# A list scheduler that tracks ScalarE's function table: an attention layer and a four-way selective scan on one core

## The chip, the core and the metric

The kernel runs on one core of one Trainium2 chip. The metric is the device time of one execution in microseconds (us). Five kinds of queues work side by side: PE (TensorE, matmuls and transposes, with its weight loads shown as PEld), DVE (VectorE), ACT (ScalarE), POOL (GpSimd), and SP, which here only issues DMAs. Each queue runs its instructions strictly in the order in which they were written, and waits on semaphores where an input or a buffer is not ready. The order in each queue is therefore the whole schedule.

## The reference, cut to what matters

Layer 0 is attention over a 256 x 256 grid of tokens with 128 channels: for each of the 256 rows, four heads of 32 channels attend along the row with a mask and a triangle bias, with a sigmoid gate, an output projection and a residual. Layer 1 is a selective scan in four directions over the same grid:

```python
xz = einsum('bhwc,ec->bhwe', x, in_proj_w); xin, z = split(xz, 2)
xc = silu(depthwise_conv3x3(xin) + conv_b)              # 256 channels
xs = [rows, columns, rows reversed, columns reversed]    # four directions k
dts_r, Bs, Cs = split(einsum('bkdl,kcd->bkcl', xs, x_proj_w))
dt = softplus(einsum('bkrl,kdr->bkdl', dts_r, dt_proj_w) + dt_proj_b)
# per direction k, channel d (256) and state n (16), along 65536 tokens:
h = h * exp(dt * A[k, d, n]) + (dt * xs) * B[n]
y = sum over n of h * C[n]
# then: sum of the directions, D * xs, layer norm, times silu(z), out_proj, residual
```

A group norm stands in front of either layer.

## The kernel before, in words

**Layer 0** works in 64 groups of 4 rows. Per row: PE makes the scores of the four heads (`scores`, L557), DVE adds the bias and takes the minimum of the negated sums (`soften`, L576), ACT takes the exponential with its row sum (`exponent`, L590), PE transposes the result (L628), ACT or DVE copies it to SBUF (L373), PE multiplies with v (L646, L651), and DVE gates (L659, L660). Per group, ACT takes one sigmoid for the gates (L509), which needs another function table than the exponential.

**Layer 1** runs the directions in the order 0, 2, 1, 3. A direction is 64 chunks of 1024 tokens, and a chunk is 32 units: 16 states times two halves of 128 channels. A unit u is:

- decay: ACT takes `exp(dt * A)` for 128 x 1024 (L1721);
- bx: `dtu * B` for each state, in eight 128 x 256 pieces a chunk and state, on ACT (L1335) or POOL (L1337), whichever is free; PE transposes the pieces into one of two PSUM buffers (`feed`, L1741);
- scan: DVE runs the recurrence over 1024 tokens (L1787);
- carry: the last state is copied out for the next chunk, on ACT (L1812) or DVE (L1814);
- hc: the states times C, on POOL or on DVE (both L1805). Which of the two is decided when the scan is placed (`choose`): if POOL's queue is short, the scan writes to SBUF and POOL multiplies ("pooled"); else the scan writes to PSUM and DVE multiplies;
- add: PE transposes the product and adds it into y (L1824); `closing` and `open_group` pass y from one group of units to the next, with a copy by ACT between them (`part`, L1377; `ys`, L1382), and sums of earlier results (`part` and `yl`, L1407).

In direction 0, half of the states instead let POOL make `xu * B` (`fill`, L1762), and ACT writes the decay to PSUM. Beside the units, each chunk has work that prepares a later chunk or finishes an earlier one: in direction 0 the convolution (L1093) and its silu (L1111); in all directions dt's projection (L1219), its softplus (L1237), transposes (L1297) and products (L1305); in direction 3 the final part: statistics (L1556, L1557), the normalisation of eight blocks on ACT (L1587) or POOL (L1592), z (L1526), its silu (L1543), the transposes of y (L1607) with their copies (`yn`, L1615), the gate's product on POOL (L1630), the output projection (L1641) and the residual (L1651).

ACT's functions lie in tables of which one is loaded at a time. A silu or softplus between decays thus costs a load before it and another before the next decay. Copies, scalings and identities need no load. The loads are not in the source; they are put in where the finished order of ACT needs them. In the source such a silu or softplus is a task of the kind `visit` (`visit1` for direction 3's silu).

The order of all queues comes from `Play`, a list scheduler that runs while the program is built. It keeps a time for each queue. `COST` gives each kind of task how long it occupies its queue and when its result is there. `pick` looks at each queue's available tasks, takes those that can start within `close` of the first, and among these the one with the smallest `due`; `step` places it. Due times are counted in units (a decay of unit u in direction 3 is due at u - 2, a feed at u - 2, and so on, from the table `TUNE`), so neither `due` nor `COST` is a time on the chip. A task with two queues (`bx` pieces, the normalisations, layer 0's copies) goes to the one where it can start first. `room` and `Lazy` bound how many buffers of a kind are in use. The tasks are only ordered by the play: on the chip each instruction starts when its queue and its semaphores allow.

Of the kernel before, what the change touches and what calls it, by code (L numbers as in the profile page):

```python
# [60 lines left out]
def _normalise(nc, out, in_, mr):  # L61
# [6 lines left out]
    "scan": (2.25, 2.34), "dve_c": (1.15, 1.23), "stat": (1.06, 1.1), "small": (0.15, 0.2),  # L68
    "add": (0.60, 0.68), "last": (0.08, 0.16),
    "decay": (1.045, 1.15), "scale": (0.402, 0.50), "carry": (0.085, 0.19), "e512": (0.47, 0.58),  # L70
    "e1024": (0.90, 1.0), "e128": (0.15, 0.25), "xn": (1.25, 1.35), "visit": (4.93, 3.62), "visit1": (4.64, 3.35), "xp": (1.05, 1.15), "dscale": (0.30, 0.40), "pool_d": (0.31, 0.36), "diag8": (1.76, 1.95),
    "norm_p": (0.91, 0.95), "give": (1.78, 1.95), "shift": (0.55, 0.65),
    "norm": (0.98, 1.1), "a512": (0.67, 0.78),
    "pool": (2.335, 2.38), "pool_s": (0.453, 0.49), "pool_x": (1.26, 1.3), "rstd": (2.0, 2.1),
    "turn8": (0.885, 1.05), "mm": (0.87, 1.05), "dp": (1.0, 1.15), "turn4": (0.45, 0.62),
    "turn_b": (0.67, 0.85), "dma": (0.36, 1.6), "dma2": (0.72, 3.2),
    "d512": (0.60, 0.69), "n512": (0.62, 0.81), "t256": (0.34, 0.42), "og": (0.76, 0.85),
    "soft": (0.85, 0.95), "exp2": (0.90, 1.0), "gate": (3.85, 2.60), "bias": (4.54, 4.55),
    "bc": (0.62, 0.70), "four": (0.95, 1.25), "dma3": (1.0, 1.6),
}  # L80


class Task:
# [3 lines left out]
class Play:  # L87
# [4 lines left out]
    def __init__(self):  # L92
        self.free_at = dict.fromkeys(self.ENGINES, 0.0)
        self.avail = {e: [] for e in self.ENGINES}
        self.close = 0.12
        self.moved = 0.0

    @staticmethod
    def after_own(d):
# [2 lines left out]
    def task(self, eng, cost, due, emit, deps=(), gate=None, more=0, lag=0.0):  # L102

        t = Task()
        t.eng = (eng,) if isinstance(eng, str) else eng
        t.cost = (cost,) if isinstance(cost, str) else cost
        t.due, t.emit, t.gate, t.after, t.by = due, emit, gate, [], None
        t.ready, t.left, t.lag = 0.0, more, lag
        for d in deps:
            if d.by is None:  # L110
                d.after.append(t)
                t.left += 1
            else:
                t.ready = max(t.ready, self.after_own(d) if t.eng == (d.by,) else d.end + SEM)
        if t.left == 0:
            self.offer(t)
        return t
# [5 lines left out]
    def sp(self, due, emit, deps=(), gate=None, cost="dma"):  # L123
        return self.task("SP", cost, due, emit, deps, gate)

    def pick(self):

        best = None
        for e in self.ENGINES:
            f, can, first = self.free_at[e], [], None  # L130
            for t in self.avail[e]:
                r = max(t.ready + t.lag if t.lag and e != t.eng[0] else t.ready, f)
                if t.gate is not None:
                    g = t.gate()
                    if g is None:
                        continue
                    r = max(r, g)
                can.append((r, t))
                first = r if first is None else min(first, r)
            if first is None or (best is not None and first > best[0]):  # L140
                continue
            due, r, t = min(
                ((t.due, r, t) for r, t in can if r <= first + self.close), key=lambda x: x[:2]
            )
            if best is None or r < best[0]:
                best = (r, t, e)
        return best

    def step(self):

        best = self.pick()
        if best is None:
            return False
        now, t, e = best
        occupied, latency = COST[t.cost[t.eng.index(e)]]
        for x in t.eng:
            self.avail[x].remove(t)
        if e == "SP":
            self.moved = max(self.moved, now + LEAD) + latency
            latency = self.moved + LAND - now  # L160
        t.by, t.fin, t.end = e, now + occupied, now + latency
        self.free_at[e] = t.fin
        t.emit(t)
        for x in t.after:
            x.left -= 1
            x.ready = max(x.ready, self.after_own(t) if x.eng == (e,) else t.end + SEM)
            if x.left == 0:
                self.offer(x)
        return True
# [563 lines left out]
def _layer1(tc, ctx, const, dram, ident, vec, mr, a, x1, x1T, out):  # L733
# [93 lines left out]
    xn = const.tile([P, LR + 2, N + 2], F32, tag="xn", name="xn")  # L827
# [8 lines left out]
    SU = ND * ST  # L836
# [25 lines left out]
    task, sp, avail, free_at = play.task, play.sp, play.avail, play.free_at  # L862
# [5 lines left out]
    def direction():  # L868
        return work[min(scanned // SU, len(work) - 1)][0]
# [4 lines left out]
    TUNE = {  # L874
        0: dict(
            w=7, hc=3, c=4, b=2, xu=3, dt=2, dtuT=1, bx=5, pull=(0.2, 1.5, 3), most=4, fills=1.5,
            calm=3, close=0.3, piece=-3.0, decay=-0.7, feed=-1, fill=-3, times=2.2, add=2.5, carry=0.8,
            early=0.0, conv=(-40.0, 5.0, 0.0), side=2.0, again=3, last=0,
            fed=(0, 2, 4, 6, 8, 10, 12, 14),
        ),  # L880
        1: dict(
            w=5, hc=4, c=5, b=3, xu=1, dt=2, dtuT=1, bx=8, pull=(-0.3, 1.5, -1), most=12, fills=2.5,
            calm=4, close=0.2, piece=-9.0, decay=-2, feed=-2, fill=-1.8, times=1.2, add=1.2, carry=1.2,
            early=0.0, conv=(-40.0, 4.5, 0.5), side=-1.0, again=0, last=0.6, fed=(), xs=1,
        ),
        2: dict(
            w=5, hc=3, c=6, b=3, xu=1, dt=2, dtuT=1, bx=8, pull=(-0.3, 1.5, -1), most=8.0, fills=4.5,
            calm=4, close=0.08, piece=-9.0, decay=-2, feed=-2, fill=-1.8, times=0.3, add=2.5, carry=0.8,
            early=0.0, conv=(-40.0, 4.5, 0.5), side=2.0, again=3, last=0, fed=(), xs=1,
        ),  # L890
        3: dict(
            w=6, hc=4, c=4, b=3, xu=1, dt=2, dtuT=1, bx=8, pull=(0.2, 1.5, -2), most=12.0, fills=5.5,
            calm=4, close=0.12, piece=-9.0, decay=-2, feed=-2, fill=-0.8, times=3, add=4, carry=1.2,
            early=0.0, conv=(-40.0, 4.5, 0.5), side=2.0, again=3, last=0.3, fed=(), xs=1,
        ),
    }
# [95 lines left out]
    def calm(u):  # L992

        def gate():
            ahead = min(u, scanned + TUNE[direction()]["calm"])
            return 0.0 if decayed >= ahead else None

        return gate
# [39 lines left out]
    def prep(i):  # L1038

        k, o, cc = chunk(i)  # L1040
        U = SU * i + TUNE[k]["side"]
# [9 lines left out]
        if k == 0:  # L1051
# [35 lines left out]
            outs = []  # L1087
            for x, j in enumerate((1, 0)):
                for q in range(QT):
# [8 lines left out]
                    def leave(pc, j=j, q=q):  # L1098
# [6 lines left out]
                        gate=xu.gate, first=xu.get, gap=c2,  # L1105
# [6 lines left out]
                        xu.half[j], xu.half[j], AF.Silu, bias=vec["conv_b"][:, j : j + 1]  # L1112
                    )

            have = [[task("ACT", "visit", U - 22, silu, outs, calm(SU * i))]] * 2
            kept = [sp(U - 18, store_xc, have[0], None, "dma2")]
            w["stores"] += kept
        else:
            xs = w["xs"] = Lazy("xs", 2, k) if k == 3 else Lent()
# [4 lines left out]
            have = [[], []]  # L1124
# [749 lines left out]
    with tc.manual_schedule():  # L1874
        n_prep, n_pieces, n_units = 0, 0, 0
        while True:
            while n_prep < len(work) and scanned >= SU * n_prep - 60:
                prep(n_prep)
                n_prep += 1
            while n_pieces < 2 * len(work) and scanned >= 16 * n_pieces - 28:  # L1880
                make_pieces(*divmod(n_pieces, 2))
                n_pieces += 1
            while n_units < min(total, scanned + 14):
                make_unit(n_units)
                n_units += 1
            play.close = TUNE[direction()]["close"]
            if not play.step():
                break
        assert scanned == total and all(x.left == 0 for x in [groups[len(work) - 1, 2]["out"]])
        assert play.done()  # L1890

@with_exitstack
def kernel(ctx: ExitStack, tc: tile.TileContext, a, out):
# [32 lines left out]
    with ExitStack() as l0:  # L1926
# [47 lines left out]
```

## Time and profile before

| what | value |
|---|---|
| median of 3 runs | 24744.65 us (24725.2 to 24746.45) |
| profiled execution | 24753.32 us, its span 24751.6 us |
| granted TensorE clock, mean | 0.982 |
| first scan of directions 0, 2, 1, 3 | at 2140.5, 8063.5, 13380.3, 18726.1 us |
| end of the last scan | 24717.1 us |
| scans (L1787) | 8192, 2.33 to 2.34 us each |
| hc on POOL and on DVE (L1805) | 6255 of 2376 ns, 1937 of 1223 ns |
| bx pieces on ACT and on POOL | 19751 of 502 ns, 8921 of 483 ns |
| decays (L1721) | 8192, 1116 to 1148 ns |
| table loads of ACT | 898 of 1283 ns |

Successive ACT instructions overlap by about 0.1 us, so 502 ns of one bx piece is about 0.40 us of ACT's time when many follow each other. A line of the profile gives the engine, the source line, what was written and read, how often, the busy time and the mean of one, and then the idle time of the engine before it with what ended it. The releaser is inferred: it is the one of several that the profile saw last, and where the named engine had long been done, it was another. A line number below is one of the kernel before; the changed kernel's are higher by 13 from `step` on.

### The profile page before, as it was taken

The page shows a single profiled execution, that of the slowest core. Times are in us where ns is not written, and L with a number is a line of the kernel's source. Part 1 is how long each engine was busy: PE and PEld are TensorE (multiplying, and loading weights), DVE is VectorE, ACT ScalarE, POOL GpSimd, SP SyncE. Part 2 cuts the span into 40 slices and gives each one's busy share as a digit, 9 for nine tenths or more (in the row PEclk, how much of TensorE's full clock was granted, in tenths as well). Part 3 has the DMA queues.
Part 4 walks back from the last instruction along what each step waited for, and adds up shares of the span by engine and source line. Part 5 has one row for each costly group of instructions (what it writes and reads, how often), then busy time and mean ns, then how long its engine had stood idle before and what let it go on. Part 6 is the DMA issues. An engine that isn't in the chain of part 4 may idle for free. (4 is left out here: it accounts for less than half of the span.)

```text
span 24751.6 us, 464821 instructions
## 1 busy us (share of the span) xinstructions
PE 23003.9 (93%) x165172; PEld 18188.1 (73%) x165172; DVE 23434.1 (95%) x19272; ACT 23427.6 (95%) x46416; POOL 23325.3 (94%) x17424
## 2 busy tenths in 40 slices
PE   8999999999999999999999999999998888888888
PEld 6666666666666788888887777777777777777777
DVE  7887999999999999999999999999999999999999
ACT  7998899999998999999999999999999999999998
POOL 5777999999999999999999999999999999999999
PEclk9999999999999999999999999999999999999999
DMA  4225777777777666666666777777775555555555
GB/s 131 90 90 171 255 259 264 259 260 262 261 259 255 233 233 225 232 228 229 231 230 232 243 245 243 244 243 244 244 243 198 180 184 178 181 182 181 185 178 168
DMA packets 2471853, 5355.13 MB, mean 216 GB/s; under 512 B 177121, under 2 KB 1366424, under 8 KB 2469528
## 3 DMA queue, kind: packets, MB, share of 16 engines
q1 hardware_dynamic: 2469240, 5324.34, 64.0%
q8 instruction: 1305, 21.38, 0.4%
q14 instruction: 1020, 8.36, 0.1%
q0 software_dynamic: 288, 1.05, 0.0%
HBM read 4846.54 MB, written 478.15 MB: 215 GB/s over the span
## 5 line engine op out<-in xcount | busy, mean ns | idle before, releaser
L1805 POOL TENSOR_TENSOR hc<-w,c 128x1024 f32<-128x1024 f32 x6255 | 14726.7, 2376 | 529.5 <-DVE w L1787 195.1
L1787 DVE TENSOR_TENSOR_SCAN w<-w,hst,s 128x1024 f32<-128x1024 f32 x5550 | 12670.6, 2329 | 295.0 <-PE s L1741 143.8
L1824 PE MATMUL y<-ident,hc 128*128 128x128 f32 x65536 | 8478.1, 277 | 520.8 <-ACT part L1377 204.8
L1741 PE MATMUL s<-ident,bx 128*128 128x128 f32 x57344 | 7713.6, 279 | 1020.7 <-DVE w L1787 662.0
L1741 PEld LDWEIGHTS s<-ident,bx 128*128 128x128 f32 x57344 | 6428.1, 142 | 3009.5 <-DVE w L1787 1289.0
L1335 ACT ACTIVATE bx<-dtuT,bT 128x256 f32<-128x256 f32 x19751 | 8578.3, 502 | 2.8 <-PE s L1741 2.5
L1824 PEld LDWEIGHTS y<-ident,hc 128*128 128x128 f32 x65536 | 7445.2, 142 | 1407.1 <-POOL hc L1805 598.2
L1721 ACT ACTIVATE w<-dt,negA 128x1024 f32<-128x1024 f32 x7168 | 8126.5, 1148 | 31.3 <-PE y L1824 15.8
L1337 POOL TENSOR_SCALAR bx<-dtuT,bT 128x256 f32<-128x256 f32 x8921 | 4103.7, 483 | 22.6 <-ACT dtuT L1034 5.9
L1787 DVE TENSOR_TENSOR_SCAN s<-w,hst,s 128x1024 f32<-128x1024 f32 x1618 | 3775.7, 2338 | 310.1 <-PE s L1741 205.7
L1805 DVE TENSOR_TENSOR hc<-s,c 128x1024 f32<-128x1024 f32 x1937 | 2366.2, 1223 | 101.6 <-DVE s L1787 27.5
L1762 POOL TENSOR_TENSOR w<-xu,b 128x1024 f32<-128x1024 f32 x1024 | 2423.2, 2372 | 0.5 <-issue 0.4
L1093 PE MATMUL cv<-xn,wtap 128*128 128x512 f32 x4608 | 2217.6, 600 | 5.5 <-ACT xn L1080 5.5
L1787 DVE TENSOR_TENSOR_SCAN w<-s,hst,w 128x1024 f32<-128x1024 f32 x705 | 1642.3, 2337 | 58.8 <-ACT s L1721 55.1
L538 POOL TENSOR_TENSOR bias<-tri,mk 128x2048 f32<-128x2048 f32 x256 | 1167.1, 4559 | 378.8 <-DVE nm L576 218.2
L1812 ACT COPY hst<-w 128x1 f32<-128x1 f32 x6255 | 1138.1, 185 | 276.7 <-DVE w L1787 244.7
L1721 ACT ACTIVATE s<-dt,negA 128x1024 f32<-128x1024 f32 x1024 | 1143.0, 1116 | 89.1 <-DVE hc L1805 88.1
L1093 PEld LDWEIGHTS cv<-xn,wtap 128*128 128x128 f32 x4608 | 790.1, 193 | 529.4 <-issue 523.2
L1219 PE MATMUL dp<-xd,dtw 8*128 8x512 f32 x2048 | 1169.4, 662 | 5.2 <-ACT xd L1189 0.9
L590 ACT ACTIVATE s<-s,nm 128x256 f32<-128x256 f32 x2048 | 1028.3, 515 | 0.8
L576 DVE CUSTOM_DVE_ANT_0 s<-sp,bias 128x256 f32<-128x256 f32 x2048 | 754.4, 415 | 69.1 <-PE sp L557 61.1
L1787 DVE TENSOR_TENSOR_SCAN s<-s,hst,w 128x1024 f32<-128x1024 f32 x319 | 745.2, 2336 | 67.4 <-POOL w L1762 67.4
(183 smaller groups left out, 19594.3 us busy)
## 6 DMA issues: line engine op xcount, KB each, us to landing
c<-xp_d SPq DMA_DIRECT2D x7040, 512.0 KB
b<-xp_d SPq DMA_DIRECT2D x896, 512.0 KB
yrow_d<-ys SPq DMA_DIRECT2D x128, 1024.0 KB
yl<-yrow_d SPq DMA_DIRECT2D x512, 256.0 KB
xc_d<-xu SPq DMA_DIRECT2D x128, 512.0 KB
yl<-xc_d SPq DMA_DIRECT2D x128, 512.0 KB
xu<-xc_d SPq DMA_DIRECT2D x128, 512.0 KB
xcT_d<-wtap SPq DMA_DIRECT2D x128, 512.0 KB
```

Of the source, the lines that this page charges most:

```text
L538: nc.gpsimd.tensor_tensor(z["bias"].get(), tri.rearrange("p b h k -> p (b h) k"), w["mk"].tile.rearrange("p (r k) -> p r k", k=N)[:, r : r ...
L1093: return lambda pc: nc.tensor.matmul(pc, wtap[:, j, t, :], xn[:, 2 * q + u : 2 * q + u + 2, v : v + N], start=t == 0, stop=t == 8,)
L1219: return lambda pt: nc.tensor.matmul(pt, dtw[:, k, j, :], xd.half[0][0:R, q * 512 : (q + 1) * 512], start=True, stop=True,)
L1335: nc.scalar.mul(dst, src, b)
L1337: nc.gpsimd.tensor_scalar(dst, src, b, 1.0, ALU.mult, ALU.mult)
L1721: nc.scalar.activation(dst, w["dt"].half[j], AF.Exp, scale=negA[:, k * ND + j, n : n + 1])
L1741: nc.tensor.transpose(dst[:, x * P : (x + 1) * P], blocks(half)[:, x, :], ident)
L1762: nc.gpsimd.tensor_tensor(box["w"].half[0], w["xu"].half[j], b_now().half[0], ALU.mult)
L1787: nc.vector.tensor_tensor_scan(rev(states), rev(a), rev(b), hst[k][:, j, n : n + 1], ALU.mult, ALU.add)
L1805: eng.tensor_tensor(box["hc"].half[0], states, c_now().half[0], ALU.mult)
L1812: nc.scalar.copy(dst, src)
L1824: nc.tensor.matmul(gr["y"][:, x, :], hc[:, x * P : (x + 1) * P], ident, is_transpose=True, start=gr["fresh"] and x == 4 * q, stop=stop and ...
```

## The change

Four things change, all of them in what the play knows and in its numbers. No operation of the reference's computation is added or removed.

1. The play keeps the table that ACT has loaded (`self.table`). `TABLE` names the table of a decay, a `visit` (softplus), a `visit0` (the convolution's silu, a new kind) and a `visit1`. Where the next task of ACT needs another table, `LOAD` = 1.41 is added to its time, and it may start that much earlier than its inputs are there.
2. The kinds `visit` and `visit1` no longer contain two loads: (4.93, 3.62) becomes (2.10, 2.21), and (4.64, 3.35) becomes (1.82, 1.93).
3. In layer 0, three kinds get other numbers: `soft` 0.85 to 0.69, `exp2` 0.90 to 0.985, `four` 0.95 to 1.07. The kind `six` is added to the table and used by no task.
4. Some due times and `close` in `TUNE` change, in each of the four directions.

```diff
-    "visit": (4.93, 3.62), "visit1": (4.64, 3.35),
+    "visit": (2.10, 2.21), "visit0": (2.10, 2.21), "visit1": (1.82, 1.93),
...
-    "soft": (0.85, 0.95), "exp2": (0.90, 1.0),
+    "soft": (0.69, 0.79), "exp2": (0.985, 1.09),
...
-    "four": (0.95, 1.25), "dma3": (1.0, 1.6),
+    "four": (1.07, 1.35), "six": (1.335, 1.6), "dma3": (1.0, 1.6),
 }
+
+LOAD = 1.41
+TABLE = {"decay": "exp", "visit": "softplus", "visit0": "silu", "visit1": "silu"}
...
         self.moved = 0.0
+        self.table = None
...
+    def load(self, e, t):
+        if e != "ACT" or TABLE.get(t.cost[t.eng.index(e)], self.table) == self.table:
+            return 0.0
+        return LOAD
+
     def pick(self):
...
                     r = max(r, g)
+                r = max(r - self.load(e, t), f)
                 can.append((r, t))
...
         occupied, latency = COST[t.cost[t.eng.index(e)]]
+        now += self.load(e, t)
...
         t.by, t.fin, t.end = e, now + occupied, now + latency
+        if e == "ACT":
+            self.table = TABLE.get(t.cost[t.eng.index(e)], self.table)
         self.free_at[e] = t.fin
...
         0: dict(
-            calm=3, close=0.3, piece=-3.0, decay=-0.7, feed=-1, fill=-3, times=2.2, add=2.5, carry=0.8,
+            calm=3, close=0.3, piece=-3.0, decay=-0.7, feed=-1.5, fill=-3, times=2.2, add=2.5,
+            carry=0.8,
...
         1: dict(
-            calm=4, close=0.2, piece=-9.0, decay=-2, feed=-2, fill=-1.8, times=1.2, add=1.2, carry=1.2,
-            early=0.0, conv=(-40.0, 4.5, 0.5), side=-1.0, again=0, last=0.6, fed=(), xs=1,
+            calm=4, close=0.2, piece=-9.0, decay=-2, feed=-2, fill=-1.8, times=2.2, add=2.5, carry=1.2,
+            early=0.0, conv=(-40.0, 4.5, 0.5), side=-1.0, again=0, last=0.3, fed=(), xs=1,
...
         2: dict(
-            calm=4, close=0.08, piece=-9.0, decay=-2, feed=-2, fill=-1.8, times=0.3, add=2.5, carry=0.8,
+            calm=4, close=0.08, piece=-9.0, decay=-2, feed=-2, fill=-1.8, times=0.3, add=3.2, carry=0.8,
...
         3: dict(
-            calm=4, close=0.12, piece=-9.0, decay=-2, feed=-2, fill=-0.8, times=3, add=4, carry=1.2,
+            calm=4, close=0.2, piece=-9.0, decay=-2, feed=-2, fill=-0.8, times=3, add=4, carry=1.2,
...
-            have = [[task("ACT", "visit", U - 22, silu, outs, calm(SU * i))]] * 2
+            have = [[task("ACT", "visit0", U - 22, silu, outs, calm(SU * i))]] * 2
```

What the two built programs hold, counted from their instruction orders:

| | before | after |
|---|---|---|
| hc on DVE, directions 0, 2, 1, 3 | 768, 342, 383, 444 | 769, 342, 384, 504 |
| bx pieces on ACT, directions 0, 2, 1, 3 | 4073, 5475, 5271, 4932 | 4079, 5478, 5190, 4448 |
| normalisations of direction 3 on ACT and on POOL | 262, 250 | 500, 12 |
| DVE's places that differ, layer 0 and directions 0, 2, 1, 3 | | 1697 of 6050; 25 of 3588; 6 of 2988; 789 of 2687; 891 of 3961 |
| table loads of ACT | 898 | 898 |

More of the change, by code (lines that the diff above doesn't have):

```diff
@@ L70 @@
     "decay": (1.045, 1.15), "scale": (0.402, 0.50), "carry": (0.085, 0.19), "e512": (0.47, 0.58),
-    "e1024": (0.90, 1.0), "e128": (0.15, 0.25), "xn": (1.25, 1.35), "visit": (4.93, 3.62), "visit1": (4.64, 3.35), "xp": (1.05, 1.15), "dscale": (0.30, 0.40), "pool_d": (0.31, 0.36), "diag8": (1.76, 1.95),
+    "e1024": (0.90, 1.0), "e128": (0.15, 0.25), "xn": (1.25, 1.35), "visit": (2.10, 2.21), "visit0": (2.10, 2.21), "visit1": (1.82, 1.93), "xp": (1.05, 1.15), "dscale": (0.30, 0.40), "pool_d": (0.31, 0.36), "diag8": (1.76, 1.95),
     "norm_p": (0.91, 0.95), "give": (1.78, 1.95), "shift": (0.55, 0.65),
@@ L77 @@
     "d512": (0.60, 0.69), "n512": (0.62, 0.81), "t256": (0.34, 0.42), "og": (0.76, 0.85),
-    "soft": (0.85, 0.95), "exp2": (0.90, 1.0), "gate": (3.85, 2.60), "bias": (4.54, 4.55),
-    "bc": (0.62, 0.70), "four": (0.95, 1.25), "dma3": (1.0, 1.6),
-}
+    "soft": (0.69, 0.79), "exp2": (0.985, 1.09), "gate": (3.85, 2.60), "bias": (4.54, 4.55),
+    "bc": (0.62, 0.70), "four": (1.07, 1.35), "six": (1.335, 1.6), "dma3": (1.0, 1.6),
+}
+LOAD = 1.41
+TABLE = {"decay": "exp", "visit": "softplus", "visit0": "silu", "visit1": "silu"}
 class Task:
@@ L876, in _layer1 @@
             w=7, hc=3, c=4, b=2, xu=3, dt=2, dtuT=1, bx=5, pull=(0.2, 1.5, 3), most=4, fills=1.5,
-            calm=3, close=0.3, piece=-3.0, decay=-0.7, feed=-1, fill=-3, times=2.2, add=2.5, carry=0.8,
-            early=0.0, conv=(-40.0, 5.0, 0.0), side=2.0, again=3, last=0,
+            calm=3, close=0.3, piece=-3.0, decay=-0.7, feed=-1.5, fill=-3, times=2.2, add=2.5,
+            carry=0.8, early=0.0, conv=(-40.0, 5.0, 0.0), side=2.0, again=3, last=0,
             fed=(0, 2, 4, 6, 8, 10, 12, 14),
```

## The prediction

> **What bounds the kernel now.** I read the page's totals first, then a table of windows cut at the first scan of each direction, then the waits of single stages, and last the timeline around the longest of those waits.
>
> ```profile
> PE 23003.9 (93%) x165172; PEld 18188.1 (73%) x165172; DVE 23434.1 (95%) x19272; ACT 23427.6 (95%) x46416; POOL 23325.3 (94%) x17424
> ```
>
> Four engines stand within 2% of each other, so no engine alone is "the" bound: a microsecond moved from one to another comes back. What can be won is idle time, and of that DVE has 24751.6 - 23434.1 = 1317 us in all. The windows (layer 0 with the start of layer 1, then directions 0, 2, 1, 3 in the order in which they run) show where it lies:
>
> ```profile
> 0.00:2140.50 2140.50, 2008.52 (x17832) 1394.76 (x17832) 1666.58 (x6050) 1870.39 (x5587) 1420.78 (x592) 0.99 0.34 99
> 2140.50:8063.50 5923.00, 5742.90 (x31957) 3968.10 (x31956) 5652.90 (x3589) 5347.45 (x9196) 5666.38 (x2460) 0.95 0.75 259
> 8063.50:13380.30 5316.80, 4974.28 (x38645) 4277.57 (x38644) 5193.14 (x2989) 5259.37 (x10278) 5223.85 (x4424) 0.99 0.69 229
> 13380.30:18726.10 5345.80, 4977.73 (x37099) 4086.75 (x37097) 5234.16 (x2688) 5230.15 (x10503) 5224.84 (x4600) 1.00 0.72 244
> 18726.10:24751.60 6025.50, 5300.51 (x39644) 4460.93 (x39644) 5687.36 (x3961) 5720.20 (x10856) 5789.49 (x5351) 0.98 0.54 180
> ```
>
> The columns after the length are busy PE, weight loads, DVE, ACT, POOL. DVE idles 270 us in direction 0, 124 in direction 2, 112 in direction 1 and 338 in direction 3. Scans follow each other in a fixed order on DVE, so a scan that starts late is the lost time. In layer 0, ACT leads: between 180 and 2060 us nearly all its idle time is the last line below, 0.97 us for each of the 64 groups. The lines before it are DVE's and POOL's waits in direction 3 (waiter, line waited for, us in total, times, longest):
>
> ```profile
> DVE s L1787 <- ACT w L1721: 100.6, 61, 1.7
> DVE w L1787 <- ACT bx L1335: 33.1, 12, 2.9
> DVE w L1787 <- ACT w L1721: 25.6, 15, 2.1
> ...
> POOL wtap L1630 <- ACT hst L1812: 94.3, 58, 2.9
> ...
> ACT e L373 <- PE pT L628: 61.9, 64, 1.8
> ```
>
> 61 times in 64 chunks is once a chunk. I numbered the scans inside a chunk 0 to 31 (S28 is scan 28, f28 the transposes of L1741 that feed it, a28 its transposes of L1824 into y, d28 its decay on ACT, h28 its product with C, c28 its carry). The 100.6 us are all at S28; 80.7 us (1.26 a chunk) are at S13, and 23.4 at S14. Here is PE, then DVE, before one S28:
>
> ```profile
> 21706.56 1.06 PE L1824 MATMUL y<-ident,hc 128*128 128x128 f32 x8 [0.43 <-ACT hst L1812]
> 21707.46 1.88 PE L1407 MATMUL y<-part,ident 128*128 128x512 f32 x4
> 21709.18 0.60 PE L1297 MATMUL dtp<-ident,dt 128*128 128x128 f32 x4
> 21709.62 1.88 PE L1407 MATMUL y<-yl,ident 128*128 128x512 f32 x4
> 21711.34 1.91 PE L1741 MATMUL s<-ident,bx 128*128 128x128 f32 x16
> ...
> 21712.47 2.35 DVE L1787 TENSOR_TENSOR_SCAN s<-w,hst,s 128x1024 f32<-128x1024 f32 x1 [1.67 <-ACT w L1721]
> ```
>
> The wait is put down to ACT, but f28 (the first half of the x16) ends at about 21712.4, right before the scan: f28 stands in PE's queue behind the part sums, a dt transpose and the yl sums. S13 has the same shape:
>
> ```profile
> 21756.43 0.99 ACT L1377 COPY part<-y 128x1024 f32<-128x1024 f32 x1
> ...
> 21757.57 1.06 PE L1824 MATMUL y<-ident,hc 128*128 128x128 f32 x8 [2.35 <-ACT part L1377]
> ...
> 21758.47 1.68 PE L1407 MATMUL y<-yl,ident 128*128 128x512 f32 x2
> ...
> 21759.93 1.91 PE L1741 MATMUL s<-ident,bx 128*128 128x128 f32 x8
> ...
> 21761.94 2.35 DVE L1787 TENSOR_TENSOR_SCAN w<-w,hst,s 128x1024 f32<-128x1024 f32 x1 [2.12 <-ACT w L1721]
> ```
>
> The part copy frees y, a8 opens it again, a yl sum goes first, then f13, then the scan.
>
> **The change part by part.** I laid the two programs' instruction orders side by side, engine by engine.
>
> *Table loads.* Both programs hold 382 loads before decays, 256 before softplus, 64 before each of the two silus: 766 in layer 1, so none is saved. A visit was played as 4.93 us; now it is 2.10 + 2 x 1.41 = 4.92. Only the second load's place differs: it is charged at the next decay, not at the visit. Row: a load takes 1283 ns and the next activation starts some 0.02 us after, so 1.41 is about right. The Trainium skill's page "ScalarE: Activation LUTs", section "What ACT_TABLE_LOAD costs", says otherwise: the load plus a drain of about 1380 ns, 2.66 us for each switch, and "Table sets: the hidden batching unit" asks to batch calls by set, which this change does not. By the page each load would be played 1.25 us short; at four loads a chunk that is 5 us x 64 = 320 us of ACT time in direction 3 that the order has no room for, and every gain below would be gone. No row of the trace shows the drain. I go by the row; the sum stands.
>
> *Directions 0 and 2: 0 us.* DVE's order differs in 25 of 3588 places in direction 0 and in 6 of 2988 in direction 2; SP's in 12 and 0. The 270 us of idle DVE in direction 0 stay. The few moved feeds and adds can cost or save 0.1 to 0.2 us a chunk; both ends are +-15 us for the two.
>
> *Direction 1: -15.* 81 scalings go from ACT to POOL (81 x 0.483 = 39 us on POOL, which idles 121; ACT gets 41 free). The products stay within one. f29 stands ahead of a27 where it stood behind; S29 loses 16.9 us now. f28 stays behind part and yl sums, so S28's 49.8 us stay. The DVE products are at other scans (3, 7, 13, 17 for 4, 10, 14, 18). With DVE 98% busy, at best all 112 us go, at worst some 40 new ones come (POOL's added work uncovered); I take the one wait that I can see leave.
>
> *Direction 3, the work.* 60 products leave POOL for DVE: +60 x 1.225 = +73.5 us on DVE, and 60 x 2.376 = 142.6 us off POOL. 484 scalings leave ACT for POOL: 243 us (at 0.502) off ACT, 234 on POOL. 238 of the 512 normalisations (L1587, L1592) move to ACT: +141 on ACT, -131 on POOL. Net: DVE +73, ACT -102, POOL -40. The DVE time is in full on the path; its hidden alternative (0, if it falls in a wait that stays) is the other bound.
>
> *Direction 3, the waits.* f28 is now in front of "DP, a24, part sums, yl sums", right behind a23; its buffer is free after S26, and S27 with its product takes 3.6 us. So S28's 100.6 us go; what is next is f29, behind the 3.8 us of sums, and c27 on ACT. I work f29 out at some 2 us before need. For S13 the order is now a8, f13, a10, yl sums: 1.7 us of sums leave the path. The part copy stands behind c10, which waits for h10; from the end of h10: two normalisations 1.1, part 1.0, a8 1.05, f13 0.95 and gaps, 4.3 us, against 2.3 + 2.3 + 1.2 = 5.9 until S13 is due. So 62 of the 80.7 us go, and I leave 19 (0.3 a chunk) for the ACT queue. S14's 23 stay: f14 now waits for c12. New products bring 60 x 0.1 = 6 us of own wait (42.5 us over 444 today). Sum: -100.6 - 62 + 73.5 + 6 = -83; say -85.
>
> *Layer 0: -30.* Three costs changed, and a quarter of the order with them; copies swap engines but balance (ACT 2 fewer of about 1300). ACT's wait of 0.97 us a group comes from PE: scores, then 1.4 us of the product with v, then the transpose that ACT needs. Now the transposes stand in front of that product. That would give 60 us. Against it: in 21 of 64 groups the second gate product stands behind the scores of the next row, and the sigmoid waits for it (a score burst is 1.15 us; from 0 to 25 us). I take half: -30, between -60 and +25.
>
> Sum: 0 - 15 - 85 - 30 = -130. From the profiled 24753.3 us (1.7 around the span) to 24623; the median of the runs shown is 8.7 lower, so 24744.65 - 130 = 24615.
>
> **The rivals.**
> *A, the waits move on.* Late feeds become late carries or late w buffers: S28's and S13's time comes back at S14, S29 or the gates, and the 73 us of products stay. Then direction 3 is between -10 and +10 and the rest gives -10 to -45: 24690 to 24745, say 24720. For it: DVE, ACT and POOL are all over 94% in the stage. Against: each wait has one named cause in the queue, and it is gone.
> *B, slower: POOL at the gate.* L1630 already waits 94.3 us. Its yn now follows normalisations that are all on ACT, the last of them behind c12. From the end of S14 I get: c14, one scaling, the copies and yn up to the second, 3.5 us. POOL idles that long and the product h14 behind it starts late. If POOL does not catch up before the chunk ends, it sets the pace: 89.8 busy + 3.4 + some 2.8 around the statistics = 96 us a chunk, against 94.15 now: +119 us, less 45 elsewhere, 24744.65 + 74 = 24819. It decides where POOL's lag at S19 exceeds about 3 us; I work out 2, as three products that follow (S16 to S18) are on DVE. POOL's 40 us less speak against it.
> *C, all of it.* Direction 3 down to 1 us of idle a chunk (-190), layer 0 -60, direction 1 -60: 24435.
> *D, it does nothing,* since the load's accounting only renames 4.93 as 4.92. Directions 0 and 2 show just that; direction 3's order is too different for it.
>
> **How the numbers follow.** Mine 0.64 (24560 to 24680), A 0.17 (0.03 of it D), B 0.11, C 0.08. A change under 0.2% (49 us, about what a measurement of this kernel can tell from none) is most of A. Faster 0.75, same 0.14, slower 0.11. The range goes from 24490 (half of C out) to 24750 (A in, B out).
>
> **What would show it.** In the profile after: S28 without its 100 us and f28 ahead of the sums; DVE's idle time in direction 3 down from 338 to some 170 with 73 more busy; directions 0 and 2 within 15 us; the 61.9 us of "e <- pT" down to half. Wrong, if direction 3 is not under 5970 us, if L1630's wait passes 200 us (B), or if directions 0 or 2 move by over 30.

## The result, and the profile after

| | us |
|---|---|
| before, median of 7 runs | 24743.59 (24725.2 to 24751.1) |
| after, median of 7 runs | 24658.46 (24650.89 to 24665.15) |
| ratio after/before, 95% interval | 0.9967 [0.9956, 0.9977] |
| predicted | 24615 (24490 to 24750) |
| profiled execution after | 24665.15, its span 24663.4 |

The change makes the kernel faster by 85 us, where 130 were forecast. First the page's totals of the changed kernel, then its windows, cut at the first scan of each direction as the prediction cut those of before (start and end, length, then busy PE, weight loads, DVE, ACT and POOL, each with its number of instructions, and last the granted TensorE clock as a share of its full rate, the share of DMA and its GB/s):

```profile
PE 23035.1 (93%) x165172; PEld 18316.0 (74%) x165172; DVE 23466.3 (95%) x19337; ACT 23337.0 (95%) x46095; POOL 23299.9 (94%) x17680
...
0.00:2155.90 2155.90, 2018.17 (x17836) 1412.01 (x17837) 1654.02 (x6052) 1875.90 (x5585) 1414.73 (x592) 0.99 0.35 99
2155.90:8081.60 5925.70, 5754.29 (x31954) 3980.40 (x31953) 5651.58 (x3591) 5344.50 (x9200) 5661.71 (x2453) 0.95 0.75 259
8081.60:13393.80 5312.20, 4971.85 (x38646) 4263.03 (x38644) 5191.91 (x2989) 5260.47 (x10278) 5225.65 (x4427) 1.00 0.69 230
13393.80:18737.60 5343.80, 4954.68 (x37099) 4090.63 (x37097) 5236.48 (x2689) 5212.63 (x10425) 5257.98 (x4671) 1.00 0.72 244
18737.60:24663.40 5925.80, 5336.06 (x39646) 4569.93 (x39644) 5732.33 (x4021) 5643.52 (x10611) 5739.84 (x5540) 0.96 0.55 183
```

Idle DVE time is the length minus its busy time. By stage:

| stage | length before | length after | difference | predicted | idle DVE before | after |
|---|---|---|---|---|---|---|
| layer 0 and start | 2140.5 | 2155.9 | +15.4 | -30 | 474 | 502 |
| direction 0 | 5923.0 | 5925.7 | +2.7 | 0 | 270 | 274 |
| direction 2 | 5316.8 | 5312.2 | -4.6 | 0 | 124 | 120 |
| direction 1 | 5345.8 | 5343.8 | -2.0 | -15 | 112 | 107 |
| direction 3 | 6025.5 | 5925.8 | -99.7 | -85 | 338 | 193 |

So direction 3 makes the whole gain, a little more than forecast, and layer 0 takes part of it back. Here are DVE's longest waits in direction 3 after, and POOL's wait for the gate:

```profile
DVE w L1800 <- PE s L1754: 51.1, 152, 4.2
DVE s L1800 <- PE s L1754: 27.9, 34, 1.2
...
POOL wtap L1643 <- ACT hst L1825: 16.2, 39, 0.7
```

The 100.6 us that came once a chunk are gone. The gate's wait is 16.2 us where it was 94.3. Summed for each scan of the chunk, DVE's idle time ahead of it went like this (us over 64 chunks of direction 3, for eight of the 32 scans):

| | S12 | S13 | S14 | S15 | S19 | S28 | S29 | S30 |
|---|---|---|---|---|---|---|---|---|
| before | 2 | 80.7 | 23.4 | 11.6 | 7.8 | 106.1 | 2.1 | 18.5 |
| after | 27.7 | 6.0 | 12.7 | 7.6 | 19.3 | 15.7 | 18.8 | 16.7 |

S13 and S28 lose 165 us; S12, S19 and S29 gain 54.

Part of these waits goes with the clock of PE. The profile records the granted TensorE clock in stretches, at 1.0 or at 0.5 of its full rate. Direction 3 has 51 stretches at 0.5 before (233 us in all) and 94 after (448 us), which makes the 0.98 of its row before and the 0.96 above. I counted a scan as having one when the stretch falls between 2 us before the scan ahead of it and its own start. Before, 98 of the 309 us of idle DVE time ahead of scans stand at such scans, 65.3 of them at S13; after, it is 76 of 163 us, and nearly all of the waits of S12 (27.5 us, 61 chunks), S14 (12.6, 27 chunks) and S19 (16.1, 28 chunks). What turns the clock down was not tested.

PE, then DVE, around one S28 of the changed kernel:

```profile
21666.13 1.04 PE L1754 MATMUL s<-ident,bx 128*128 128x128 f32 x8
21667.10 1.12 PE L1232 MATMUL dp<-xd,dtw 8*128 8x512 f32 x2
21668.15 1.09 PE L1837 MATMUL y<-ident,hc 128*128 128x128 f32 x8
21669.08 1.88 PE L1420 MATMUL y<-part,ident 128*128 128x512 f32 x4
21670.80 1.88 PE L1420 MATMUL y<-yl,ident 128*128 128x512 f32 x4
21672.52 1.04 PE L1754 MATMUL s<-ident,bx 128*128 128x128 f32 x8
...
21669.82 2.35 DVE L1800 TENSOR_TENSOR_SCAN s<-w,hst,s 128x1024 f32<-128x1024 f32 x1
21673.66 2.35 DVE L1800 TENSOR_TENSOR_SCAN w<-w,hst,s 128x1024 f32<-128x1024 f32 x1 [0.24 <-ACT hst L1825]
```

f28 (21666.13) is now ahead of the sums (21669.08), and S28 starts with no wait. f29 (21672.52) is the one behind the sums, and it ends at 21673.56, just as S29 is due: the next late thing is named, and here it costs 0.24 us.

In layer 0, ACT's waits between 180 and 2077 us:

```profile
ACT e L386 <- PE pT L641: 44.3, 96, 1.6
ACT qT L471 <- PE pq L464: 18.8, 23, 0.8
ACT v L386 <- PE pv L488: 7.3, 24, 0.3
```

The wait for the transpose fell from 61.9 us to 44.3, but it comes 96 times instead of 64, and two waits are new. Of the copies of the queries (qT), ACT makes 85 where it made 4, and they wait for PE. From 180 us to 2060 before and to 2076 after, ACT's idle time went from 73.0 to 84.1 us and its busy time from 1807.0 to 1811.9.

### The profile page after: what moved, and what is told of

Same layout as the page of the kernel before. It is cut to its first block, busy times and chain, and to the rows that moved or that the text cites. A ratio compares the mean times of both kernels' runs of the same rounds, so it can differ in the third digit from the quotient of the medians.

```text
span 24663.4 us, 465342 instructions
## 1 busy us (share of the span) xinstructions
PE 23035.1 (93%) x165172; PEld 18316.0 (74%) x165172; DVE 23466.3 (95%) x19337; ACT 23337.0 (95%) x46095; POOL 23299.9 (94%) x17680
## 5 line engine op out<-in xcount | busy, mean ns | idle before, releaser
L1800 DVE TENSOR_TENSOR_SCAN w<-w,hst,s 128x1024 f32<-128x1024 f32 x5493 | 12536.5, 2329 | 282.3 <-PE s L1754 156.8
L1348 ACT ACTIVATE bx<-dtuT,bT 128x256 f32<-128x256 f32 x19195 | 8349.3, 502 | 3.1 <-PE s L1754 2.8
L1350 POOL TENSOR_SCALAR bx<-dtuT,bT 128x256 f32<-128x256 f32 x9477 | 4362.5, 484 | 24.6 <-DVE dtuT L1318 8.7
L1800 DVE TENSOR_TENSOR_SCAN s<-w,hst,s 128x1024 f32<-128x1024 f32 x1675 | 3910.1, 2339 | 186.8 <-PE s L1754 173.7
L1818 DVE TENSOR_TENSOR hc<-s,c 128x1024 f32<-128x1024 f32 x1999 | 2440.5, 1222 | 88.6 <-DVE s L1800 25.2
```

Of the source, the lines that this page charges most:

```text
L1348: nc.scalar.mul(dst, src, b)
L1350: nc.gpsimd.tensor_scalar(dst, src, b, 1.0, ALU.mult, ALU.mult)
L1800: nc.vector.tensor_tensor_scan(rev(states), rev(a), rev(b), hst[k][:, j, n : n + 1], ALU.mult, ALU.add)
L1818: eng.tensor_tensor(box["hc"].half[0], states, c_now().half[0], ALU.mult)
```

## The experiments

All ratios are to the kernel before, run beside the experiment on the same chip. "Stages" are the lengths of layer 0 and of directions 0, 2, 1, 3.

### Layer 0's costs put back

```diff
-    "soft": (0.69, 0.79), "exp2": (0.985, 1.09),
+    "soft": (0.85, 0.95), "exp2": (0.90, 1.0),
-    "four": (1.07, 1.35),
+    "four": (0.95, 1.25),
```

> The changed kernel with the three layer-0 costs of before (soft 0.85, exp2 0.90, four 0.95). Layer 0's order is then that of before in every place, layer 1's that of the changed kernel. My theory: the changed kernel's first scan of direction 0 came 15.4 us later (2155.9 against 2140.5) because of layer 0's order alone, so here it comes at 2140 to 2142 and the time is about 24658 - 15 = 24643. Rival: the start of layer 1 is late for another reason (its own first chunk): then the first scan stays at 2155 and the time at 24658.

Measured: 24635.43 us, ratio 0.9959 [0.9947, 0.9972]. Stages 2139.5, 5924.2, 5307.0, 5343.3, 5926.3. Layer 0 is back at its old length and direction 3 stays. So the 15 us of layer 0 come from its own order, and the three new costs there are a loss. Which of the three makes it was not tried.

### The tracking alone

The kernel before with the table tracking, the new costs of the visits and `visit0`, but with the old `TUNE` and the old layer 0.

> The kernel before with the tracking of the table alone (LOAD, TABLE, the new visit costs, visit0); due times, close and layer 0's costs as before. Direction 3's order differs from before in 9 DVE places of 3961 only, f28 is again behind the part and yl sums. My theory (the searched due times and close make the gain, not the tracking): direction 3 stays at 6015 to 6030 us and scan 28 waits about 100 us in all; direction 1's order is new (352 products on DVE for 383) and gives +-40 us; the time is 24700 to 24785. Rival (the tracking makes the gain): direction 3 at about 5926 and the time at about 24645.

Measured: 24757.44 us, 1.0007 [0.9998, 1.0016]. Stages 2137.2, 5919.2, 5313.6, 5446.6, 5929.2. No difference in sum, but not for want of effect: direction 3 is 96 us shorter, where 6015 to 6030 us were expected, and direction 1 is 101 us longer. In direction 3 only 9 of DVE's places differ from before. S13's wait falls from 80.7 to 3.2 us there, and S28's stays:

```profile
DVE s L1800 <- ACT w L1734: 92.4, 57, 1.7
```

The difference ahead of S13 begins on ACT. After the final part's silu (L1543; L1556 with the tracking), ACT ran the carries c6 and c7 and then pieces of bx. Before:

```profile
21743.04 1.92 ACT L1543 ACTIVATE wtap<-wtap 128x2048 f32<-128x2048 f32 x1
21744.87 0.17 ACT L1812 COPY hst<-w 128x1 f32<-128x1 f32 x1
21747.27 0.16 ACT L1812 COPY hst<-s 128x1 f32<-128x1 f32 x1 [2.23 <-DVE hc L1805]
21747.35 1.31 ACT L1335 ACTIVATE bx<-dtuT,bT 128x256 f32<-128x256 f32 x3
21748.68 1.28 ACT L1721 ACT_TABLE_LOAD   x1
```

With the tracking alone:

```profile
21787.47 1.92 ACT L1556 ACTIVATE wtap<-wtap 128x2048 f32<-128x2048 f32 x1
21789.29 0.49 ACT L1348 ACTIVATE bx<-dtuT,bT 128x256 f32<-128x256 f32 x1
...
21791.29 0.16 ACT L1825 COPY hst<-s 128x1 f32<-128x1 f32 x1 [1.02 <-DVE hc L1818]
...
21792.28 1.28 ACT L1734 ACT_TABLE_LOAD   x1
```

And in the whole change:

```profile
21700.97 1.92 ACT L1556 ACTIVATE wtap<-wtap 128x2048 f32<-128x2048 f32 x1
21702.79 0.89 ACT L1348 ACTIVATE bx<-dtuT,bT 128x256 f32<-128x256 f32 x2
...
21704.88 0.17 ACT L1825 COPY hst<-w 128x1 f32<-128x1 f32 x1
21705.08 1.28 ACT L1734 ACT_TABLE_LOAD   x1
```

Before, the old play thought that ACT was loading a table at this place (the visit held both loads), so it put the carries first; on the chip the load comes only ahead of the next decay, and ACT stood idle for 2.23 us until c7 could run. Then the load, the decays, the `part` copy and a8 were late: in the two chunks shown, a8 starts 17.71 us after S6 before and 16.49 us after it with the tracking. With the tracking, pieces of bx fill the time and the wait for c7 is 1.02 us. In the whole change S7 is pooled (c7 reads w, not s), so nothing is waited for. Mean idle time of ACT between this silu and the next load, against S13's wait:

| kernel | idle ACT, us a chunk | S13, us |
|---|---|---|
| before | 1.89 | 80.7 |
| f28 first (below) | 1.87 | 89.3 |
| tracking alone | 1.00 | 3.2 |
| due times alone | 0.70 | 6.1 |
| whole change | 0.02 | 6.0 |
| normalisations on POOL (below) | 0.69 | 44.9 |

ACT's idle time alone does not give S13's wait: the last row has little of it and 44.9 us. The clock of PE is the other part. Here is the same place in another chunk of the kernel before (PE, then DVE), and then the windows of the clock, first of this chunk, then of the one that the prediction shows at 21757 to 21762 us:

```profile
22504.83 1.07 PE L1824 MATMUL y<-ident,hc 128*128 128x128 f32 x8 [2.03 <-ACT part L1377]
22505.73 1.02 PE L1407 MATMUL y<-yl,ident 128*128 128x512 f32 x2
22506.59 1.04 PE L1741 MATMUL s<-ident,bx 128*128 128x128 f32 x8
...
22507.72 2.35 DVE L1787 TENSOR_TENSOR_SCAN w<-w,hst,s 128x1024 f32<-128x1024 f32 x1 [0.31 <-issue]
...
22505.00:22508.40 3.40, 3.40 (x27) 2.87 (x26) 3.09 (x3) 3.40 (x9) 3.40 (x4) 1.00 0.91 263
21758.70:21762.10 3.40, 3.40 (x13) 2.39 (x12) 1.28 (x2) 3.40 (x7) 3.40 (x4) 0.50 0.67 185
```

The order is the same, and PE has waited some 2 us ahead of a8 in both. At the full clock the yl sum took 1.02 us and f13 1.04, and S13 waited 0.31 us; in the prediction's chunk, at half the clock, they took 1.68 and 1.91, and S13 waited 2.12. Over direction 3 before, S13 waits 2.18 us on average in the 30 chunks with a stretch at 0.5 ahead of it (65.3 us) and 0.45 us in the 34 without (15.4 us). My estimate from these means: 52 of the 80.7 us, (2.18 - 0.45) x 30, are the slower clock, and 29 are the lateness that came from ACT. With the tracking alone PE waits 0.94 us ahead of a8 where it waited 2.04 on average, 4 chunks have such a stretch, and S13 hardly waits. With the normalisations on POOL, 35 chunks have one and hold all of the 44.9 us. So a shorter wait of PE and fewer stretches at half the clock go together in the tracking kernel; that the one brings the other was not tested. PE's order there still has the yl sum ahead of f13, as before.

In direction 1 the same tracking does harm. S28's waits there are 132.7 us (49.8 before), nearly all in this line:

```profile
DVE s L1800 <- ACT w L1734: 127.7, 62, 2.6
```

PE's order there is f27, eight transposes of dt, a24, the part and yl sums, then f28, so f28 is late again; the profile names ACT's decay.

### The due times alone

The kernel before with the new `TUNE`; the visits, the load and layer 0 as before.

> The kernel before with the table TUNE of the changed kernel alone; visits contain their two loads as before, layer 0's costs as before. f28 stands ahead of the sums, 504 products of direction 3 are on DVE, 378 of its normalisations on ACT (262 before, 500 after). My theory: most of the gain is here: direction 3 at 5920 to 5960, directions 0, 2, 1 within 10 us of the changed kernel's, layer 0 at 2140, time 24640 to 24690. Rival (the tracking makes the gain): direction 3 over 6000, time over 24715.

Measured: 24599.20 us, 0.9943 [0.9931, 0.9956]: the fastest of all, 36 us under the experiment with tracking, due times and old layer 0 in the same series (24635.43). Stages 2140.5, 5912.6, 5309.5, 5349.5, 5885.4: against that experiment 41 us less in direction 3 and 12 in direction 0, and 9 more in directions 2 and 1. It was expected at 24640 to 24690. Its direction 3 and DVE's longest waits there:

```profile
18712.10:24597.50 5885.40, 5328.64 (x39645) 4561.33 (x39644) 5723.51 (x4021) 5640.28 (x10611) 5760.15 (x5539) 0.97 0.55 184
...
DVE w L1787 <- PE s L1741: 18.2, 22, 2.3
DVE s L1787 <- PE s L1741: 17.5, 31, 1.1
```

Idle DVE time is 162 us against 193 in the whole change. So with these due times the tracking is not needed, and costs 36 us. The orders differ in this: here f28 stands directly ahead of a24 and the sums ("f27, four dt transposes, a23, four dt transposes, f28, a24, part sums, yl sums"); in the whole change all eight dt transposes are ahead of a23, and a dt projection stands between f28 and a24. S28 waits 8.2 us here and 15.7 in the whole change, S30 1.1 and 16.7. In the whole change PE also stands idle ahead of the second four dt transposes, for ACT's copy of bT: 56.3 us in 60 times in direction 3, and here no such wait is listed. Neither the projection nor this copy was tested by itself.

### One due time: the sums half a unit later

The kernel before; in direction 3 the part sums and the last yl sums are due half a unit later.

```diff
-            made = adds(name, due + 7, [t], lambda: own)
+            made = adds(name, due + 7 + (0.5 if k == 3 and e == 2 else 0), [t], lambda: own)
-            made = adds("part", U + 26, [groups[i, 0]["out"]], lambda: w["part"])
+            made = adds("part", U + 26 + (0.5 if k == 3 else 0), [groups[i, 0]["out"]], lambda: w["part"])
```

> The kernel before with one due time moved in direction 3 alone: the part sums and the last yl sums (L1407) half a unit later, so that they no longer tie with f28. Layer 0 and directions 0, 2 and 1 keep the order of before in every place. The order of direction 3 follows: f28 ahead of the sums, f13 ahead of the yl sums, 465 products on DVE, 380 normalisations on ACT. My theory (the two waits of scans 28 and 13 are PE's queue): scan 28's 106 us and most of scan 13's 81 go, direction 3 at 5900 to 5950, time 24640 to 24690. Rival (the wait at scan 28 is ACT's late decay, as the profile names it): the wait stays near 100 us and direction 3 over 6000.

Measured: 24853.14 us, 1.0045 [1.0031, 1.0058], slower, where 24640 to 24690 us were expected. Direction 3 is 6127.6 us. S28 falls to 42.7 us, but S19 waits 109.8, S18 48, S1 37.8, S29 30.5. Of these waits 108.0 us at S19 (40 chunks) and 36.8 at S1 (20 chunks) stand behind stretches at half the clock, which make 660 us of this direction. The due time changed the order of direction 3 on all engines (465 products on DVE for 444), so this run is no test of f28's place: it shows only that a due time in this play moves much of what comes after it.

### f28 ahead of the sums, and nothing else

The kernel before with the play unchanged; when it comes to the sums of direction 3 ahead of f28, they are held and written right behind f28. Only 256 instructions of PE move (and some of SP's); DVE, ACT and POOL keep their order in every place.

```diff
-        t.emit(t)
+        if t.mark is not None and t.mark[0] == "sum" and t.mark[1] not in self.fed:
+            self.held.append(t)
+        else:
+            t.emit(t)
+        if t.mark is not None and t.mark[0] == "feed":
+            self.fed.add(t.mark[1])
+            for x in self.held:
+                x.emit(x)
+            self.held = []
...
+            if u % SU == 28 and k in (3,):
+                f.mark = ("feed", i)
```

> The kernel before with 256 instructions of PE moved and nothing else of the compute queues: in direction 3 the part sums and the last yl sums (L1407) stand behind f28 and not ahead of it. My theory (f28's place in PE's queue is the wait of scan 28): the 106 us at scan 28 fall under 20, direction 3 goes from 6025 to 5925-5945 us and the time from 24739 to 24640-24670. Rival 1 (the wait is the decay on ACT that the profile names): nothing changes, 24730 to 24745. Rival 2 (the time comes back at the next feeds, as in the run with one due time moved): direction 3 at 5990 to 6030.

Measured: 24767.86 us, 1.0014 [1.0005, 1.0023], where 24640 to 24670 were expected. Direction 3 is 6041.5 us, 16 longer than before. S28's wait falls from 106.1 us to 1.6, so f28's place was its cause, whatever name the profile gives. But S30's goes from 18.5 to 156.4 and S29's from 2.1 to 12.3. One chunk, PE then DVE:

```profile
21715.83 1.04 PE L1753 MATMUL s<-ident,bx 128*128 128x128 f32 x8
21716.71 1.88 PE L1417 MATMUL y<-part,ident 128*128 128x512 f32 x4
21718.42 1.88 PE L1417 MATMUL y<-yl,ident 128*128 128x512 f32 x4
21720.14 1.04 PE L1753 MATMUL s<-ident,bx 128*128 128x128 f32 x8
21721.01 2.78 PE L1838 MATMUL y<-ident,hc 128*128 128x128 f32 x24
21723.63 0.60 PE L1514 MATMUL x3p<-ident,xt 128*128 128x128 f32 x4
21724.07 1.04 PE L1838 MATMUL y<-ident,hc 128*128 128x128 f32 x8
21724.94 0.60 PE L1514 MATMUL x3p<-ident,xt 128*128 128x128 f32 x4
21725.38 1.91 PE L1753 MATMUL s<-ident,bx 128*128 128x128 f32 x16
...
21718.03 2.35 DVE L1801 TENSOR_TENSOR_SCAN s<-w,hst,s 128x1024 f32<-128x1024 f32 x1
21726.51 9.06 DVE L1801 TENSOR_TENSOR_SCAN w<-w,hst,s 128x1024 f32<-128x1024 f32 x4 [2.56 <-ACT hst L1826]
```

The scan at 21718.03 is S28, with no wait; the one at 21726.51 is S30 with 2.56 us. The profile names the carry c28 for it, which frees f30's PSUM buffer and stands on ACT behind twelve pieces of bx:

```profile
21719.52 4.89 ACT L1345 ACTIVATE bx<-dtuT,bT 128x256 f32<-128x256 f32 x12
21724.31 0.14 ACT L1826 COPY hst<-s 128x1 f32<-128x1 f32 x1
```

But f30 (the first half of the last x16) starts 0.93 us after c28's end, and PE did not wait for it: between f28 and f30 PE works without a pause on the sums, f29, four adds (L1838) and two groups of transposes (L1514), and in none of the 64 chunks does it pause there. Moving f28 ahead of the sums leaves the work ahead of f30 the same, so DVE meets PE's queue two scans later. c28 stands next in the way: it ends at 21724.45, and S30 could have started at 21723.95.

### The tracking with f28 ahead of the sums

The same hold on top of the tracking alone, in directions 1 and 3 (512 of PE's places).

```diff
+            if u % SU == 28 and k in (1, 3):
+                f.mark = ("feed", i)
```

> The tracking alone (LOAD, TABLE, visit costs; due times and layer 0 as before) with the same move of the sums behind f28, in directions 1 and 3: 512 instructions of PE. My theory: scan 28 loses its 133 us in direction 1 and its 105 us in direction 3 nearly whole, so 24757 - 200 to 230 gives 24530 to 24560: the tracking's loss was f28 behind the sums. Rival (the tracking's direction 1 is slow for its softplus one unit later): direction 1 stays over 5400 and the time over 24620.

Measured: 24710.65 us, 0.9991 [0.9982, 1.0000]. Direction 1 is 5387.8 us, 59 shorter than with the tracking alone: S28 falls from 132.7 us to 2.3, and S30 rises from 2.5 to 64.7. Here the carry does hold f30: PE waits for ACT's carry between S28 and S30 in 62 chunks, 54.8 us in all. Direction 3 is 5941.5 us, 12 longer, with S30 at 158.4 and again PE's own queue ahead of f30. The expectation of 24530 to 24560 failed: f28 alone hands all of its wait on in direction 3 and about half in direction 1.

### The normalisations on POOL only

The whole change with layer 0 put back, and

```diff
-        nm = [task(("ACT", "POOL"), ("norm", "norm_p"), U + 10 + x, norm(x), [mrs]) for x in range(4)]
+        nm = [task(("POOL",), ("norm_p",), U + 10 + x, norm(x), [mrs]) for x in range(4)]
```

> The changed kernel with layer 0's costs of before and with the 512 normalisations of direction 3 on POOL alone (500 on ACT in the changed kernel). The order of direction 3 follows: 445 products on DVE, 3006 bx pieces on POOL, f28 behind the sums again, f13 ahead of the yl sums. My theory: scan 28's wait is back at about 100 us and scan 13's is not; direction 3 at 5930 to 6030, time 24640 to 24740. Rival (the normalisations on ACT delay yn and leave POOL idle at the gate, L1630): POOL's wait there falls well under that of the changed kernel and direction 3 goes below 5926.

Measured: 24718.69 us, 0.9994 [0.9984, 1.0004], no difference from before; direction 3 is 6012.4 us, with 445 products on DVE. The gate's wait on POOL:

```profile
POOL wtap L1643 <- DVE w L1800: 78.1, 58, 2.8
```

With the normalisations on ACT it is 16.2 us, so there they do not delay the gate; with them on POOL the wait is back. But f28 stands behind the sums again in this kernel (S28 88.4 us), as expected, and S13 waits 44.9 us, which was not expected, so neither the gate's wait nor the 86 us that direction 3 takes over the kernel with layer 0 put back can be put to the normalisations alone.

### A load planned at 2.66 us

The whole change with layer 0 put back and the price of a load raised to what the Trainium skill's page "ScalarE: Activation LUTs" gives in "What ACT_TABLE_LOAD costs" for a switch.

```diff
-LOAD = 1.41
+LOAD = 2.66
```

> The changed kernel with layer 0's costs of before and LOAD = 2.66 for 1.41: the play leaves a whole switch of 2.66 us before an activation with another table. Theory (a load costs 1283 ns and 20 ns of gap, as in every row of the trace): ACT is played 1.25 us too busy at each of 766 loads, work goes to POOL and DVE that ACT had room for (517 products of direction 3 and 444 of direction 1 on DVE, for 504 and 384), and the time rises by 50 to 200 us over 24635. Rival (a switch costs 2.66 us in all): the order fits the chip better and the time falls below 24620; ACT's idle time would shrink by 1 us a load.

Measured: 25066.44 us, 1.0135 [1.012, 1.015], 431 us over the kernel with layer 0 put back, where 50 to 200 were expected. Stages 2139.0, 5988.8, 5328.6, 5506.7, 6086.2. In the page's rows of this kernel the loads before decays, and direction 3:

```profile
L1734 ACT ACT_TABLE_LOAD x382 | 490.1, 1283 | 6.6
...
18963.10:25049.20 6086.10, 5404.93 (x39636) 4565.08 (x39636) 5783.47 (x4033) 5546.90 (x10325) 5870.81 (x5835) 0.96 0.54 178
```

The loads still take 1283 ns, while ACT idles 6086.1 - 5546.9 = 539 us in this direction against 282 in the whole change: the play left room for a drain that the loads of this kernel do not show, and gave POOL and DVE more work. In the whole change the next instruction of ACT starts 0.03 us after a load on average, over all 898. No run here shows the drain.

## Why the prediction was right or wrong

**Layer 0 (-30): wrong.** The step was "the transposes stand in front of that product. That would give 60 us ... I take half". Part of it is seen (61.9 to 44.3 us), but I wrote "copies swap engines but balance" and counted them at nothing. They balance in busy time (+5 us), and not in waits: the query copies that came to ACT (4 to 85) wait 18.8 us for PE and those of v another 7.3. The sign of the step failed, within its bound of +25. Putting the costs back returned 16 us of the stage (2155.9 to 2139.5), and 18 us of the time when each kernel is taken against the runs of before beside it. The step is off by 45 us, and the whole forecast by 43 (24658.46 - 24615): that the other misses cancel is luck.

**Table loads ("none is saved", 0): right in the count, wrong in what followed.** The loads are the same 898 of 1283 ns, and the row and not the page's 2.66 us was right, as the run with 2.66 shows. But I took the renaming for harmless ("only the second load's place differs") and gave rival D for directions where little moved. The tracking alone gives 96 us in direction 3, where it moves 9 places of DVE, and takes 101 in direction 1, where it moves many more.

**S13 (-62): the size was right, the cause was not, and that is luck.** I put it to the 1.7 us of yl sums ahead of f13. The tracking kernel keeps a yl sum there and S13's wait is 3.2 us. Two things stand in its place: ACT idle for 2.23 us at c7 after the silu, which made the part copy late, and the clock of PE, granted at half in 30 of the 64 chunks. The prediction's own lines have the second, and I did not read it: f13 takes 1.91 us for eight transposes there, where I reckoned 0.95, and the 1.7 us of the sum are 1.02 at the full clock. The trace of before also has the carries among ACT's waits of direction 3 (for DVE's products, 204.2 us in 159 times; 157.7 in 225 times after). The gain was 75 us, S14 gave another 11 ("S14's 23 stay"), and 26 came back at S12.

**S28 (-100.6): right in cause and size, and short by one step.** f28 was ahead and 90 of 106 us went. "What is next is f29" holds too (S29 2.1 to 18.8). But f28 alone is worth nothing in direction 3: the run that moved it and nothing else lost all of it at S29 and S30, where PE's queue had the same work ahead of f30. The change keeps the gain in an order that differs in more than f28: f30 stands ahead of a26 and a28 where it stood behind both. Which of the other moves are needed was not separated.

**Direction 3's work (+73.5 on DVE): mis-sized.** DVE's busy time rose by 45.0 us. The products are as forecast (543.8 to 615.7, +71.9); a row that I did not look at fell (the last statistics, `mrs`, from 30.5 to 14.8 us), and the rows of the scans and of dt's products fell by 6.6 and 3.5. ACT fell by 77 us where -102 was worked out, POOL by 50 where -40. DVE's idle time there fell by 145 us, where -157 was worked out. Direction 3 in sum: -99.7, not -85 (my terms add up to -83).

**Direction 1 (-15): -2.0.** The step "f28 stays behind part and yl sums, so S28's 49.8 us stay" was wrong (15.0), S29's 16.9 fell to 2.4 as said, and a wait of 35.5 us at S5 and 11.2 at S12 took their place. So S28 and S29 gave up 49 us together, and DVE's idle time fell by 4.

**Directions 0 and 2: +2.7 and -4.6**, inside the +-15 given.

**The rivals.** B, POOL at the gate, did not occur (16.2 us against the 94.3 of before, not over 200). A, the waits move on, holds for direction 1 and for f28 alone in direction 3, but not for the change in direction 3. C did not come.

**What stays open.** Which of the three layer-0 costs makes the 15 us; what in the order with tracking costs 36 us against the due times alone; which moves beside f28's the gain in direction 3 needs; and what turns PE's clock down, which goes with 76 of the 163 us that DVE still waits ahead of scans in direction 3.

## What to carry to other kernels

Where queues run in order, a wait ahead of a scan is priced by following each instruction back through its own queue, all of them, and not only the one that the profile names: the late S13 began on ACT, two copies after a silu. Before a PE wait is put to the order, the duration of its instructions should be compared between chunks: the same f13 took 1.04 us at the full clock and 1.91 at half. Taking one late instruction forward gives back nothing if the work ahead of the next one stays the same (f28 alone: S28 -105 us, S30 +138), so a single move should be costed together with the next feeds behind it. A truer price is not by itself a gain, since prices and due times act together: the best kernel here, at 24599 us, has the new due times and the old prices.

## What the runs showed of the hardware

- The granted TensorE clock was 1.0 or 0.5. In direction 3 of the kernel before, the same sum and the same f13 took 1.02 and 1.04 us at 1.0, 1.68 and 1.91 us at 0.5, and S13 waited 0.45 us on average without a stretch at 0.5 ahead of it and 2.18 us with one.
- The profile put S28's wait to ACT's decay (100.6 us before, 92.4 with the tracking alone). Moving PE's f28 and nothing on ACT took it away. It put S30's wait in that run to ACT's carry, and PE came to f30 only 0.93 us after the carry's end, without having paused.
- A table load took 1283 ns in every kernel, 382 times before a decay, with 6.6 us of idle time in all ahead of them in the kernel planned at 2.66 us.
